# Moving the attention block's fold and raising its DVE steps in a fused attention and convolution kernel

## The chip, the cores and the metric

The kernel runs on one core of a Trainium2 chip. The metric is device microseconds of one execution of the whole program. Five engines work side by side, each on its own list of instructions in a fixed order: TensorE (PE, with the weight loads shown apart as PEld), VectorE (DVE), ScalarE (ACT), GpSimd (POOL) and SyncE (SP, which issues most of the DMAs). An instruction that waits for a semaphore holds up all that stands behind it in its engine's list.

## The reference

`x` is 8 images of 384 channels and 64 by 64 tokens, float32. Two layers follow each other, each with a residual:

```python
def _L0_conv_ref(x, Wq, bq, Wk, bk, Wv, bv, Wfc, bfc):
    q = apply_rope_2d(conv1x1(x, Wq, bq))
    k = apply_rope_2d(conv1x1(x, Wk, bk))
    v = conv1x1(x, Wv, bv)
    q = jax.nn.elu(to_heads(q) * scale) + 1.0          # 6 heads of 64
    k = jax.nn.elu(to_heads(k)) + 1.0
    kv = jnp.einsum('bhnd,bhne->bhde', k, to_heads(v))
    k_sum = k.sum(axis=2)
    normalizer = jnp.einsum('bhnd,bhd->bhn', q, k_sum)[..., None]
    out = jnp.einsum('bhnd,bhde->bhne', q, kv) / (normalizer + 1e-06)
    return conv1x1(out, Wfc, bfc)
...
x = x + _L0_conv_ref(_gn(x), ...)   # group norm, 32 groups, no affine part
x = x + _L1_conv_ref(_gn(x), ...)   # 1x1, filter on 8x8 FFT patches, depthwise 3x3, gelu gate, 1x1
```

## The kernel before

An image `b` is worked on in 8 bands `j` of 512 tokens; a band is a tile of 128 partitions by 3 channel tiles by 512. Two stages alternate. In the first, `queries(b, ...)`, the attention of image `b` is finished: for each band `q_project` makes the queries (matmuls `pq` L599, rotation on DVE L611, L626, L628, then elu as two activations on ACT L337, L338 and a DVE step L339), `q_normalise` multiplies them with the key sums (`pn` L637) and inverts (DVE L645, L646, and a split in two bfloat16 parts by ACT casts L650, L652 and DVE L651, L653), `q_spread` brings the inverse to all channels (`prb` L661) and multiplies it in (DVE L670, four steps for a band), and `project_out` multiplies with the folded matrix `mt` (`pf` L678) and adds to `x` (L682). In the second stage, the loop over bands of layer 1, the keys and values of image `b + 1` are projected and summed up in the accumulator `acc` (L470) in between the matmuls of layer 1, so that at its end `acc` holds the sum of key times value, and the sum of keys, of every head. The last band's depthwise taps of the image before (`late`, ACT L780, DVE L799, contraction L832, L843) run inside `queries`.

What is called the block here is `kv_finish_heads` (images 1 to 7): it reads `acc`, copies the key sums out (L567), has POOL spread them into `ks_bd` (`key_sums`, twelve copies L498), writes `kvt_bd` by six DVE steps (L572), two for each of three channel tiles, turns the three tiles on PE (`pt` L584), copies the result to `kvt` on ACT (L585) and, in `fold`, multiplies with `wfc` (`pm` L508); nine ACT copies (L515) then place it in `mt`. Image 0 has a function of its own, `kv_finish`, with other steps before the same `fold`; there four of the nine copies are on DVE (L513).

`kv_finish_heads` is a generator. `queries` steps it once after each third of band 1's query projection (the order of the three `pq` is 2, 0, 1), and then has

```python
        next(late, None)
        if b:
            run(finish)
        normalise(0)
        run(q_project(b, 2, wq, qbias, q))
```

so that `pn` of band 0 is recorded behind the fold. Later `normalise(j + 1)` stands between the projections of band `j + 2`. A third chain, `layer0_chain(b + 1, ...)`, is stepped once or twice for every band: it is the group norm of the next image, whose steps are small matmuls (`ps_m`, `ps_mc`, `ps_v`, `ps_r`, L273 and L281) and small DVE steps on 32 partitions (L301, L304, L307 to L310 make `rsg`, which `ps_r` reads). It runs for images 1 to 7, during the queries of images 0 to 6.

The order of the instructions on each engine is made when the program is built: a scheduler goes by the recorded order and by priorities, and inside `with tc.high_priority():` an instruction goes ahead of others that are ready. PSUM is one pool of eight banks, so a matmul group also waits for the last reader of the bank it gets.

Of the kernel before, what the change touches and what calls it, by code (L numbers as in the profile page):

```python
# [12 lines left out]
ALU = mybir.AluOpType  # L13

P = 128
C = 384
CT = 3
# [6 lines left out]
HD = 64  # L24
# [93 lines left out]
def conv_blocks_kernel(ctx: ExitStack, tc: tile.TileContext, a: dict, out: bass.AP, nb: int):  # L118
    nc = tc.nc
# [9 lines left out]
    def ps_tile(name):  # L129
        return psum.tile([P, 512], F32, tag="ps", name=name)  # L130

    def w_tile(shape, name):
        return work.tile(shape, F32, tag="w", name=name)
# [6 lines left out]
    def load_x(b, j):  # L140
        if b >= nb:
            return
        t = xp.tile([P, CT, BT], F32, tag="x", name=f"x_{b}_{j}")
        nc.sync.dma_start(t, x_in[b][:, :, j * BT : (j + 1) * BT])
        xt[b, j] = t
# [102 lines left out]
    halves = (slice(0, 64), slice(64, P))  # L248
# [3 lines left out]
    kvt_bd = const.tile([P, CT, P], F32, tag="kvt_bd", name="kvt_bd")  # L252
# [239 lines left out]
    def key_sums(kx, column):  # L492

        for c0, at, n in QRUNS:

            for s in range(0, n, 32):
                h, c, q = (c0 + s) // HD, c0 + s, at + s
                nc.gpsimd.tensor_copy(  # L498
                    ks_bd[q % P : q % P + 32, q // P, h : h + 2 * NH + 1 : NH],
                    kx[c % P : c % P + 32, c // P, column : column + 1].to_broadcast([32, 3]),  # L500
                )

    def fold(b, kvt, wfc, done):

        mt = small.tile([P, CT, C], F32, tag="mt", name=f"mt_{b}", bufs=1)
        for t in range(CT):
            pm = ps_tile(f"pm_{b}_{t}")
            nc.tensor.matmul(pm[:, :C], kvt[:, t, :], wfc[:, t, :], start=True, stop=True)  # L508
            for i, (c, at, n) in enumerate(QPIECES):
                if c // P == t:  # L510
                    dst, src = mt[at % P : at % P + n, at // P, :], pm[c % P : c % P + n, :C]
                    if i % 2 and not b:
                        nc.vector.tensor_copy(dst, src)  # L513
                    else:
                        nc.scalar.copy(dst, src)  # L515
        done.append(mt)
# [46 lines left out]
    def kv_finish_heads(b, acc, vb, wfc, done):  # L563

        kx = acc[:, : CT * (HD + 1)].rearrange("p (m d) -> p m d", m=CT)
        sums = small.tile([P, CT, 1], F32, tag="key_sums", name=f"key_sums_{b}")
        nc.vector.tensor_copy(sums, kx[:, :, HD:])  # L567
        key_sums(sums, 0)
        for m in range(CT):
            for h in range(2):  # L570
                head = 2 * m + h
                nc.vector.scalar_tensor_tensor(  # L572
                    kvt_bd[halves[h], m, halves[h]],
                    vb[halves[h], head * HD : (head + 1) * HD],
                    kx[halves[h], m, HD : HD + 1],
                    kx[halves[h], m, :HD],
                    ALU.mult,
                    ALU.add,
                )
        yield  # L580
        kvt = w_tile([P, CT, P], f"kvt_{b}")
        pt = ps_tile(f"pt_{b}")
        for m in range(CT):
            nc.tensor.transpose(pt[:, m * P : (m + 1) * P], kvt_bd[:, m, :], ident)  # L584
        nc.scalar.copy(kvt, pt[:, : CT * P].rearrange("p (m k) -> p m k", m=CT))  # L585
        yield
        yield
        fold(b, kvt, wfc, done)

# [42 lines left out]
    def q_normalise(b, j, q):  # L632

        pn = ps_tile(f"pn_{b}_{j}")
        for t in range(CT):
            for s in range(4):
                nc.tensor.matmul(  # L637
                    pn[32 * s : 32 * s + 32, :P],
                    ks_bd[:, t, :],
                    q[:, t, s * P : (s + 1) * P],  # L640
                    start=(t == 0),
                    stop=(t == CT - 1),
                )
        rn = small.tile([P, P], F32, tag="rn", name=f"rn_{b}_{j}")
        nc.vector.tensor_scalar_add(rn, pn[:, :P], 1e-6)  # L645
        nc.vector.reciprocal(rn, rn)  # L646

        part = small.tile([P, P], BF16, tag="part", name=f"part_{b}_{j}")
        parts = small.tile([P, P], BF16, tag="parts", name=f"parts_{b}_{j}")
        nc.scalar.copy(part, rn)  # L650
        nc.vector.scalar_tensor_tensor(rn, part, take_off[:, 0:1], rn, ALU.mult, ALU.add)  # L651
        nc.scalar.copy(part, rn)  # L652
        nc.vector.scalar_tensor_tensor(parts, part, take_off[:, 1:2], rn, ALU.mult, ALU.add)  # L653
        return parts

    def q_spread(b, j, q, rn):
        pr = [ps_tile(f"prb_{b}_{j}_{s}") for s in range(4)]
        for t in range(CT):
            for s in range(4):
                strip = slice(32 * s, 32 * s + 32)  # L660
                nc.tensor.matmul(  # L661
                    pr[s][:, t * P : (t + 1) * P],
                    expand[strip, t * P : (t + 1) * P],
                    rn[strip, :],
                    start=True,
                    stop=True,
                )
        for s in range(4):
            qq = q[:, :, s * P : (s + 1) * P]
            nc.vector.tensor_mul(qq, qq, pr[s][:, :C].rearrange("p (t n) -> p t n", t=CT))  # L670
# [196 lines left out]
    def layer0_chain(b, prepared):  # L867

        if b >= nb:
            return  # L870
        wk = load_weight(b, "wk", k_runs) if b else first_wk
        params = []
        if b == 0:
            sum_weight(wk, "wk")
        yield from norm_chain(b, 0, params)
        scale_weight(wk, params)
        yield
        prepared += params, wk, k_bias(b, params)
# [5 lines left out]
    def run(*chains):  # L884

        chains = list(chains)
        while chains:
            chains = [c for c in chains if next(c, chains) is not chains]
# [65 lines left out]
    def queries(b, keys, before_last, late):  # L954


        wq, qbias = keys.wq, keys.qbias
        q, done, normaliser = {}, [], {}

        def normalise(j):  # L960
            normaliser[j] = q_normalise(b, j, q[j])

        run(q_project(b, 0, wq, qbias, q))
        before_last()
        run(keys.accumulate(NBAND - 1))
        next(late, None)
        finish = keys.finish(done)
        for _ in zip(q_project(b, 1, wq, qbias, q), finish):
            pass
        prepared = []  # L970
        chain = layer0_chain(b + 1, prepared)

        next(late, None)
        if b:
            run(finish)
        normalise(0)
        run(q_project(b, 2, wq, qbias, q))
        run(finish)
        mt = done[0]
        q_spread(b, 0, q[0], normaliser.pop(0))  # L980
        project = q_project(b, 3, wq, qbias, q)
        next(project)
        normalise(1)
        run(project)
        run(project_out(b, 0, q.pop(0), mt))
        q_spread(b, 1, q[1], normaliser.pop(1))
        normalise(2)
        for j in range(2, NBAND):
            if j < NBAND - 2:
                project = q_project(b, j + 2, wq, qbias, q)  # L990
                for _ in range(2):
                    next(project)
                normalise(j + 1)
                run(project)
                next(chain, None)
            q_spread(b, j, q[j], normaliser.pop(j))
            output_ = project_out(b, j - 1, q.pop(j - 1), mt)
            if j == NBAND - 2:
                next(output_)
                normalise(j + 1)  # L1000
            run(output_)
            if j < NBAND - 2:
                next(chain, None)
            if j in (5, 7):
                load_x(b + 1, j // 6)
            next(late, None)
        run(chain)
        run(project_out(b, NBAND - 1, q.pop(NBAND - 1), mt))
        return prepared
# [24 lines left out]
    take_off = const.tile([P, 2], F32, tag="take_off", name="take_off")  # L1034
# [62 lines left out]
    before_last, late = nothing, iter(())  # L1097
    for b in range(nb):
        prepared = queries(b, keys, before_last, late)
        keys = Keys(b + 1, prepared)  # L1100
        params = []
# [16 lines left out]
        for j in range(NBAND):  # L1118
# [5 lines left out]
            h = normalised(b, j, params, (8, 8), "f") if j else ahead  # L1124
# [26 lines left out]
        def before_last(b=b):  # L1151
            contract(b, NBAND - 2)
# [6 lines left out]
    h = ahead  # L1159
    for j in range(NBAND):  # L1160
# [4 lines left out]
        if j < NBAND - 1:  # L1165
            h = normalised(b, j + 1, params, (8, 8), "f")
# [52 lines left out]
```

## Time and profile before

| | |
|---|---|
| time, median of 3 runs | 3357.73 us (3355.45 to 3360.14) |
| the profiled execution's own time | 3356.93 us |
| its span in the profile | 3354.8 us |
| mean granted clock of PE | 0.994 |
| busy: PE, DVE, ACT | 98%, 82%, 61% of the span |

A row of the timeline gives the start and the length of an instruction, or of a run of like ones, in us from the start of the span, then the engine, the line, what is written and read, the size and the count; brackets give the idle time ahead of it and what ended it. A float32 matmul leaves two records, so `x6` is one group of three. A row's length includes some 0.1 us that the next instruction already overlaps, so steps are better taken from start to start. The granted clock is the share of its full clock that PE was given.

### The profile page before, as it was taken

To read this page: it belongs to the slowest core of one execution; us is meant where nothing else is said; L and a number is where in the kernel's file an instruction comes from. 1 tells how busy PE (TensorE), PEld (TensorE's weight loads), DVE (VectorE), ACT (ScalarE), POOL (GpSimd) and SP (SyncE) were. 2 spreads that over 40 slices of the span, in tenths; PEclk is the share of its full clock that TensorE was granted. 3 is DMA by queue.
4 is the path that set the end of the run, shared out by engine and by line. 5 is a ranking of instruction groups with operands and counts; after the bars stand their busy time and mean duration, and the time that the engine had idled before them with its cause. 6 is when DMAs were issued, how large, how long until landed. Compare 5 with 4: busy or idle time off the path is not lost.

```text
span 3354.8 us, 53523 instructions
## 1 busy us (share of the span) xinstructions
PE 3293.9 (98%) x21370; PEld 1850.3 (55%) x21370; DVE 2752.8 (82%) x4524; ACT 2032.8 (61%) x4032; POOL 134.2 (4%) x261
## 2 busy tenths in 40 slices
PE   8999999999999999999999999999999999999987
PEld 5544566456654566545665456654566445664454
DVE  7577789967889688896888968898788977989698
ACT  4445666566665566655666656656576665556563
POOL 0000000000010000100001000000000000000000
PEclk9999999999999999999999999999999999999999
DMA  6323335342443423534335343443333431324113
GB/s 223 107 95 99 95 80 128 110 137 67 109 113 113 137 67 95 129 110 120 86 83 133 108 121 76 103 132 107 103 96 95 133 117 52 86 70 126 58 25 52
DMA packets 151502, 343.37 MB, mean 102 GB/s; under 512 B 27365, under 2 KB 38613, under 8 KB 143061
## 3 DMA queue, kind: packets, MB, share of 16 engines
q1 hardware_dynamic: 123844, 282.85, 25.1%
q0 software_dynamic: 27216, 56.89, 11.3%
q8 instruction: 168, 2.75, 0.3%
q14 instruction: 82, 0.66, 0.1%
q10 hardware_dynamic: 192, 0.21, 0.0%
HBM read 232.70 MB, written 99.88 MB: 99 GB/s over the span
## 4 chain that ended last, share of the span: by engine, by line
PE 78%; DVE 14%; ACT 5%; issue 2%; DMA 0%; SPq 0%; DVEq 0%; ACTq 0%
PE pk L438 14%; PE pi L696 14%; PE pf L678 13%; PE pv L454 13%; PE pq L599 7%; DVE dw L799 5%; PE pw L832 4%; PE pb L731 3%; PE pd L710 2%; PE pw L843 2%; PE acc L470 2%; PE acc L483 2%; DVE qc L611 1%; ACT qs L620 1%; DVE qs L611 1%
## 5 line engine op out<-in xcount | busy, mean ns | idle before, releaser
L799 DVE SCALAR_TENSOR_TENSOR dw<-ring,w_dw,dw 128x512 f32<-128x512 f32 x1401 | 977.9, 747 | 244.5 <-ACT ring L747 205.4
L438 PE MATMUL pk<-wk,x 128*128 128x384 f32 x1536 | 544.1, 495 | 0.0
L599 PE MATMUL pq<-x,wq 128*128 128x512 f32 x1152 | 524.7, 603 | 2.6 <-ACT mt L515 2.6
L696 PE MATMUL pi<-w_in,hf 128*128 128x384 f32 x1536 | 514.8, 492 | 1.3 <-ACT hf L332 1.3
L678 PE MATMUL pf<-qc,mt 128*128 128x512 f32 x1152 | 510.7, 597 | 0.0
L454 PE MATMUL pv<-wv,x 128*128 128x384 f32 x1344 | 470.0, 488 | 0.0
L696 PEld LDWEIGHTS pi<-w_in,hf 128*128 128x128 f32 x1536 | 288.6, 191 | 196.1 <-issue 4.1
L438 PEld LDWEIGHTS pk<-wk,x 128*128 128x128 f32 x1536 | 283.1, 190 | 204.8 <-issue 31.6
L461 ACT COPY v<-pv 128x384 f32<-128x384 f32 x224 | 108.7, 485 | 424.5 <-PE pv L454 423.3
L678 PEld LDWEIGHTS pf<-qc,mt 128*128 128x128 f32 x1152 | 214.3, 190 | 255.5 <-issue 243.4
L454 PEld LDWEIGHTS pv<-wv,x 128*128 128x128 f32 x1344 | 253.6, 190 | 181.4 <-issue 8.4
L599 PEld LDWEIGHTS pq<-x,wq 128*128 128x128 f32 x1152 | 210.9, 191 | 247.1 <-issue 227.0
L682 DVE SCALAR_TENSOR_TENSOR x<-pf,bfc,x 128x512 f32<-128x512 f32 x192 | 139.0, 745 | 92.3 <-PE pf L678 92.1
L337 ACT ACTIVATE qs<-qc 128x512 f32<-128x512 f32 (+1 forms) x128 | 107.0, 836 | 171.3 <-DVE qc L628 171.3
L179 ACT ACTIVATE differences<-x,shift 128x512 f32<-128x512 f32 x168 | 120.2, 716 | 120.6 <-DVE x L682 120.6
L832 PE MATMUL pw<-gated,w_out 128*128 128x256 f32 x768 | 179.4, 383 | 0.0
L441 DVE TENSOR_TENSOR kc<-pk,kbias 128x384 f32<-128x384 f32 x256 | 140.8, 550 | 39.3 <-PE pk L438 39.2
L703 ACT COPY ht<-pi 128x384 f32<-128x384 f32 x256 | 115.1, 482 | 91.6 <-PE pi L696 88.2
L832 PEld LDWEIGHTS pw<-gated,w_out 128*128 128x128 f32 x768 | 146.7, 192 | 37.1 <-issue 6.5
L337 ACT ACTIVATE ks<-kc 128x1536 f32<-128x1536 f32 x64 | 95.0, 1485 | 98.5 <-DVE kc L445 97.7
L862 POOL DMA_DIRECT2D out_dram<-y x63 | 80.7, 1280 | 1811.2 <-ACT y L857 1004.7
L332 ACT ACTIVATE hf<-x,nb,rs 128x512 f32<-128x512 f32 x192 | 146.4, 808 | 2.4 <-DVE nb L315 2.3
(178 smaller groups left out, 4407.2 us busy)
## 6 DMA issues: line engine op xcount, KB each, us to landing
tq<-in_tq SPq DMA_DIRECT2D x64, 1024.0 KB, 4.8
x<-in_x SPq DMA_DIRECT2D x64, 768.0 KB, 6.0
tk<-in_tk SPq DMA_DIRECT2D x64, 768.0 KB, 4.4
out_dram<-x SPq DMA_DIRECT2D x63, 768.0 KB, 3.3
out_dram<-y POOLq DMA_DIRECT2D x63, 768.0 KB, 7.8
xs<-in_x SPq DMA_DIRECT2D x56, 768.0 KB, 5.8
dw<-tap POOLq DMA_DIRECT2D x14, 512.0 KB, 7.4
wk<-in_wk SPq DMA_DIRECT2D x8, 576.0 KB, 3.9
```

Of the source, the lines that this page charges most:

```text
L179: nc.scalar.activation(out[:, m, :], x_[:, m, :], AF.Identity, bias=shift[:, m : m + 1], accum_out=of_m[0])
L332: nc.scalar.activation(dst, src, AF.Identity, bias=nb_[:, t : t + 1], scale=rs[:, t : t + 1])
L337: nc.scalar.activation(e, x_, AF.Relu, scale=-1.0)
L438: nc.tensor.matmul(pk[:, :C], tokens(t), wks[:, t, :], start=(t == 0), stop=(t == CT - 1))
L441: nc.vector.tensor_add(kc[:, i, :], pk[:, :C], bias)
L454: nc.tensor.matmul(pv[:, :C], xt[b, j][:, t, i * P : (i + 1) * P], wvs[:, t, :], start=(t == 0), stop=(t == CT - 1),)
L599: nc.tensor.matmul(p_, wqs[:, t, m * P : (m + 1) * P], xt[b, j][:, t, :], start=(t == 0), stop=(t == CT - 1),)
L678: nc.tensor.matmul(p_, mt[:, t, m * P : (m + 1) * P], q[:, t, :], start=(t == 0), stop=(t == CT - 1))
L682: nc.vector.scalar_tensor_tensor(xm, p_, bfc[:, m : m + 1], xm, ALU.add, ALU.add)
L696: nc.tensor.matmul(p_[:, :C], h[:, t, i * P : (i + 1) * P], w_in[:, t, :], start=(t == 0), stop=(t == CT - 1),)
L799: nc.vector.scalar_tensor_tensor(acc[:, m], src, wd, acc[:, m], ALU.mult, ALU.add)
L832: nc.tensor.matmul(p_[h][:, m - m0, :], w_out[:, 0, m * P : (m + 1) * P], gated[:, h * HT : (h + 1) * HT], start=(m == m0), stop=False,)
```

## The change

Three things are changed. In `kv_finish_heads` the six steps L572 are recorded ahead of the POOL copies and get the highest priority, and one `yield` moves from behind the transpositions to ahead of them, so that `pt` is recorded after all three `pq` of band 1. In `q_normalise` the two DVE steps of the inverse, and the casts and steps of its split, get the highest priority, for every band of every image. In `queries`, `normalise(0)` is recorded ahead of `run(finish)`, and so ahead of the fold.

```diff
         sums = small.tile([P, CT, 1], F32, tag="key_sums", name=f"key_sums_{b}")
         nc.vector.tensor_copy(sums, kx[:, :, HD:])
+        with tc.high_priority():
+            for m in range(CT):
+                for h in range(2):
+                    head = 2 * m + h
+                    nc.vector.scalar_tensor_tensor(
+                        kvt_bd[halves[h], m, halves[h]],
...
+                    )
         key_sums(sums, 0)
-        for m in range(CT):
-            for h in range(2):
...
+        yield
         yield
         kvt = w_tile([P, CT, P], f"kvt_{b}")
         pt = ps_tile(f"pt_{b}")
         for m in range(CT):
             nc.tensor.transpose(pt[:, m * P : (m + 1) * P], kvt_bd[:, m, :], ident)
         nc.scalar.copy(kvt, pt[:, : CT * P].rearrange("p (m k) -> p m k", m=CT))
-        yield
         yield
         fold(b, kvt, wfc, done)
...
         rn = small.tile([P, P], F32, tag="rn", name=f"rn_{b}_{j}")
-        nc.vector.tensor_scalar_add(rn, pn[:, :P], 1e-6)
-        nc.vector.reciprocal(rn, rn)
-
+        with tc.high_priority():
+            nc.vector.tensor_scalar_add(rn, pn[:, :P], 1e-6)
+            nc.vector.reciprocal(rn, rn)
         part = small.tile([P, P], BF16, tag="part", name=f"part_{b}_{j}")
         parts = small.tile([P, P], BF16, tag="parts", name=f"parts_{b}_{j}")
-        nc.scalar.copy(part, rn)
-        nc.vector.scalar_tensor_tensor(rn, part, take_off[:, 0:1], rn, ALU.mult, ALU.add)
-        nc.scalar.copy(part, rn)
-        nc.vector.scalar_tensor_tensor(parts, part, take_off[:, 1:2], rn, ALU.mult, ALU.add)
+        with tc.high_priority():
+            nc.scalar.copy(part, rn)
+            nc.vector.scalar_tensor_tensor(rn, part, take_off[:, 0:1], rn, ALU.mult, ALU.add)
+            nc.scalar.copy(part, rn)
+            nc.vector.scalar_tensor_tensor(parts, part, take_off[:, 1:2], rn, ALU.mult, ALU.add)
         return parts
...
         next(late, None)
+        normalise(0)
         if b:
             run(finish)
-        normalise(0)
         run(q_project(b, 2, wq, qbias, q))
```

## The prediction

> **What bounds the kernel now.** I read the page first: PE is busy all the time, so only time in which PE waits can be won, and whatever makes PE wait is paid in full.
>
> ```profile
> PE 3293.9 (98%) x21370; PEld 1850.3 (55%) x21370; DVE 2752.8 (82%) x4524; ACT 2032.8 (61%) x4032; POOL 134.2 (4%) x261
> ```
>
> Then PE's list of waits (total us, times, longest). The change aims at the first and third of these rows, 14.3 us together; the second belongs to the group norm chain, and it will matter.
>
> ```profile
> PE pt L584 <- DVE kvt_bd L572: 9.7, 13, 1.3
> PE ps_r L281 <- DVE rsg L310: 5.2, 9, 2.4
> PE prb L661 <- DVE parts L653: 4.6, 7, 0.7
> PE pq L599 <- ACT mt L515: 2.6, 1, 2.6
> ```
>
> Third, PE's timeline where image 1's block lies. Images 2 to 6 repeat it to 0.1 us every 408.3 us.
>
> ```profile
> 582.49 5.42 PE L599 MATMUL pq<-x,wq 128*128 128x512 f32 x12
> 587.74 0.27 PE L584 MATMUL pt<-groups,kvt_bd 128*128 128x128 f32 x1
> 589.28 0.33 PE L584 MATMUL pt<-groups,kvt_bd 128*128 128x128 f32 x1 [1.27 <-DVE kvt_bd L572]
> 589.91 0.33 PE L584 MATMUL pt<-groups,kvt_bd 128*128 128x128 f32 x1 [0.29 <-DVE kvt_bd L572]
> 590.07 2.74 PE L599 MATMUL pq<-x,wq 128*128 128x512 f32 x6
> 592.65 2.10 PE L508 MATMUL pm<-wfc,kvt 128*128 128x384 f32 x6
> 594.68 0.86 PE L637 MATMUL pn<-qc,ks_bd 128*32 128x128 f32 x24
> 595.47 7.99 PE L599 MATMUL pq<-x,wq 128*128 128x512 f32 x18
> ...
> 612.67 2.74 PE L678 MATMUL pf<-qc,mt 128*128 128x512 f32 x6
> ```
>
> Last, the DVE and PE timelines where the group norm chain of the next image ends, and the granted clock in two windows after image 0's wait of 2.58 us. The columns of a window are busy time by engine, then PE's clock (0.88, 0.81).
>
> ```profile
> 664.23 0.29 DVE L645 TENSOR_SCALAR rn<-pn 128x128 f32<-128x128 f32 x1 [1.32 <-PE pn L637]
> ...
> 666.77 0.14 DVE L310 TENSOR_TENSOR rsg<-rsg,y 32x1 f32<-32x1 f32 x1
> 666.83 0.33 DVE L651 SCALAR_TENSOR_TENSOR rn<-part,take_off,rn 128x128 f32<-128x128 bf16 x1
> 667.10 0.73 DVE L611 SCALAR_TENSOR_TENSOR qs<-pq,qbias,tq 128x512 f32<-128x512 f32 x1
> 667.76 0.33 DVE L653 SCALAR_TENSOR_TENSOR parts<-part,take_off,rn 128x128 bf16<-128x128 bf16 x1
> 668.02 0.67 DVE L626 TENSOR_TENSOR qs<-qs,sq 128x512 f32<-128x512 f32 x1
> ```
> ```profile
> 666.96 0.60 PE L281 MATMUL ps_r<-rsg,of_group 32*128 32x1 f32 x4
> ```
> ```profile
> 200.00:203.00 3.00, 0.42 (x12) 0.19 (x2) 2.91 (x6) 2.90 (x5) 0.00 (x0) 0.88 0.40 164
> 203.00:210.00 7.00, 7.00 (x14) 3.06 (x15) 6.46 (x14) 1.54 (x4) 0.00 (x0) 0.81 0.00 0
> ```
>
> **The order that the change makes.** I compared the orders of the two built programs, engine by engine. No matmul is added or removed. In images 1 to 7 PE's order pq, pq, pt, pq, pm, pn becomes pq, pq, pq, pt, pn, pm. DVE does all six L572 ahead of L339 (128x1024). ACT casts `part` in between the copies of `mt`, and does band 1's elu behind all nine copies. On SP one load changes places with a neighbour in each image; POOL's order stays.
>
> **Part 1, the wait at pt: gain.** PE ends the second pq at 587.65 (twelve records of 0.43). The third pq then runs at once (2.58), then pt (0.57 with its gaps: pt starts at 590.32 and ends for the next at 590.80). L572 is done by 586.78 + 6 x 0.30 = 588.6, so nothing is waited for. pn takes 0.79 to 591.59; its inputs, L339 (588.6 + 1.23) and POOL's twelve copies (586.93 + 3.56 = 590.49), are there. The copy of kvt on ACT (0.48 from 590.97) is hidden by pn. pm takes 2.03, so band 2's pq starts at 593.65 instead of 595.47: -1.82 for each of images 1 to 6. In image 7 pt starts at 3037.69 and the pq after it at 3038.70, a wait shorter by 1.3, so -0.5 there. The first prb waited some 0.26 for parts: gone as well.
>
> **Part 2, what is late next: band 0's pf.** It needs all four L670 of band 0. ACT works without a gap from the end of pt, by its rows from start to start: kvt 0.50, two L620 1.41, four mt copies 1.94, tap 0.66, part 0.32, tap 0.66, mt 0.49, part 0.32, four mt 1.94, L620 0.71, L337 0.66, L620 0.70, L338 0.54, L337 1.08, L338 1.06. That is 12.99: band 1's elu input is ready at 590.97 + 12.99 = 603.96, against 600.59 before. DVE waits too: L645 now stands behind one L611 and waits for pn (from 590.4 to 591.7), with the rest of band 1's rotation queued behind it, on which ACT's elu waits; and the two part steps wait for the casts. So L339 of band 1 ends at 605.23. PE would be at band 1's pn at 606.62 - 2.08 = 604.54 and waits 0.75. DVE goes on: L339 1.14, two L611 1.32, two L628 1.74, L645 0.20, L670 0.47, L646 0.86, L670 0.47, L339 0.60, to 610.80; the next L339 needs ACT's last L338 of band 2, at 610.85 (L628's end 608.28, then 0.97, 0.54, 1.06); then L339 1.14, L651 0.26, L670 0.50, L653 0.26, L670 0.55 end at 613.59. PE is ready for pf at 605.29 + 0.79 + 5.26 = 611.34 and waits 2.26. pf starts at 613.6 instead of 612.67: what pt gave is gone, and 0.93 more. Bounds: if ACT and DVE were quick enough, 0; if each cast costs one further step of 0.66 to 0.75, 3.7 in all. I keep 2.26, which is made of rows.
>
> **Part 3, the later steps.** Parts of band 2 are ready at some 626.9 (L646 now runs from 623.7), and prb wants them at 631: its wait of 0.65 goes, in images 1 to 7. The load of band 3's `tq` waits for the last L611 of band 1, now near 598.2; it is needed at 613.5, and the issue table has 4.8 us to landing. The tap on POOL is 3 us later, and its readers come after 640.
>
> **Part 4, ps_r: loss.** In images 1 to 6 L645 of band 5 now stands ahead of L304, and L651, one L611, L653 and L626 ahead of L309 and L310. L645 still waits for pn at 664.23. So rsg comes later by L304 0.06, L651 0.27, L611 0.66, L653 0.26, L626 0.60: 1.85. PE stands at ps_r, with prb and pf behind it, where it waited 0.1 to 0.2 already: +1.85 in each of six images. In image 0 the order differs by one step, and PE's next pq (2.58) covers that.
>
> The Trainium skill ("VectorE: DVE Perf Modes", The DRAIN you can't avoid) has every DVE step followed by a flush of about its length less 266 ns. The rows differ: L611 is 0.74 long and the next starts 0.66 later. By the page part 4 would be some 3 us an image; the rows decide.
>
> **Part 5, image 0.** By the same walk L645 of band 1 frees a bank at 201.8, where PE waited for a copy of mt until 202.81, and pf starts near 207.8 instead of 209.49: -1.7, which includes the slow clock after the old wait (twelve pq took 6.84 instead of 5.42).
>
> **The sum.** Images 1 to 6: -1.82 - 0.26 + 0.75 + 2.26 - 0.65 + 1.85 = +2.13 each, 12.8. Image 7, without part 4: -0.5 - 0.26 + 0.75 + 2.26 - 0.65 = +1.6. Image 0: -1.7. Together +12.7.
>
> **The clock.** The two windows say that a wait of 2.58 us cost 1.42 more. In layer 1 of the last image PE waits of 2.14, 2.28, 2.57 and 3.52 us are followed by such stretches, one of 1.99 is not, nor are the 1.27 and 0.29 at pt. My thirteen new waits are 2.0 (ps_r) and 2.26 (pf), at the edge. Bounds 0 and 13 x 1.42 = 18.5; I take none at ps_r, nearest to 1.99, and three of seven at pf, nearest to 2.14 and 2.28 but between large matmuls: +4.3.
>
> The skill ("TensorE: Matmul & The Clock Gate", Why this matters for your kernels) sets the limit at idle gaps of about 3 us, which leaves this term at 0. The row after 2.58 us speaks against it.
>
> So 12.7 + 4.3 = 17.0 on the profiled execution's 3356.93 is 3373.9; the median before lies 0.8 higher, and the forecast is 3374.7. A difference within 0.2% (6.7 us) is about what a measurement of this kernel can't tell from no change.
>
> **The rivals.**
> - *No wait at pf* (the faster one). If the last L670 ends before 611.3, ACT's chain being shorter by 2.3, images 1 to 6 have -1.82 - 0.26 - 0.65 + 1.85 = -0.88, image 7 -1.4, image 0 -1.7: -8.4, 3349. For it: ACT is busy only 61% of the span. Against: every item of its chain is a row, and it has no gap. 0.07.
> - *No loss at ps_r*: 12.7 - 11.1 = +1.6, 3359. It needs rsg's steps to run ahead, against the built order. 0.07.
> - *Neither*: -8.4 - 11.1 = -19.5, 3338. The change would do just what its words say. 0.04.
> - *Most new waits slow the clock*: ten or more of thirteen, +14 to +18 instead of +4.3: 3385 to 3389. 0.08.
> - *The forecast*, both waits and none to nine slow stretches: 3370 to 3383, and from 3366 where the wait at pf is 0.6 shorter in each of seven images: 0.74.
>
> The range 3359 to 3384 takes in the forecast and the second rival. Faster by over 0.2% is the first and third rivals, 0.11; within 0.2% is the second and the forecast's low edge, 0.10; slower 0.79.
>
> **What would show it.** In the changed profile: no wait of PE at pt; waits near 0.7 at band 1's pn and 2.3 at band 0's pf on L670 (seven times); none at prb; waits near 2.0 at ps_r, six times; in image 0 the wait for mt shorter. If pf shows no wait, part 2 is wrong; if ps_r keeps 0.2, part 4 is; if all stand and the time is under 3366 or over 3384, the clock is.

## The result, and the profile after

The changed kernel takes 3382.7 us (median of 6 runs, 3377.9 to 3384.3), the kernel before 3357.97 beside it: a ratio of 1.0071, 95% interval 1.0058 to 1.0084. It is slower by 0.7%. The profiled execution took 3382.57 us (before: 3356.93), its span is 3380.8 us, the mean granted clock 0.990 (before: 0.994).

The page's first part shows the same instructions on every engine, and 11 us more of busy time on PE, with no matmul added: some matmuls took longer.

```profile
PE 3305.1 (98%) x21370; PEld 1853.4 (55%) x21370; DVE 2755.2 (81%) x4524; ACT 2030.9 (60%) x4032; POOL 134.7 (4%) x261
```

PE's list of waits (total, times, longest) has lost pt and prb, which the change aimed at, and has gained pf and pn; ps_r's total has tripled. These three rows hold 34.7 us; the rows pt, ps_r and prb of before held 19.5.

```profile
PE ps_r L281 <- DVE rsg L310: 15.3, 13, 1.9
PE pf L680 <- DVE qc L672: 14.8, 7, 2.1
...
PE pn L638 <- DVE qc L339: 4.6, 7, 0.7
```

PE's timeline at image 1's block. (Lines from L584 on stand one or two lower in the changed file: L680 is pf, L672 the spread's multiplication, L663 prb, L638 pn, L600 pq, L586 pt.) The block itself now runs through without a wait, as it was meant to. The waits come later, at band 1's pn and band 0's pf.

```profile
579.74 7.99 PE L600 MATMUL pq<-x,wq 128*128 128x512 f32 x18
587.57 0.49 PE L586 MATMUL pt<-groups,kvt_bd 128*128 128x128 f32 x3
587.99 0.86 PE L638 MATMUL pn<-qc,ks_bd 128*32 128x128 f32 x24
588.78 2.20 PE L508 MATMUL pm<-wfc,kvt 128*128 128x384 f32 x6
...
602.42 0.86 PE L638 MATMUL pn<-qc,ks_bd 128*32 128x128 f32 x24 [0.66 <-DVE qc L339]
603.21 5.42 PE L600 MATMUL pq<-x,wq 128*128 128x512 f32 x12
610.74 7.96 PE L680 MATMUL pf<-qc,mt 128*128 128x512 f32 x18 [2.11 <-DVE qc L672]
```

The same pf, 18 records of the same shape after the same wait, one image later, and the pf behind image 1's wait at ps_r: 9.66 and 9.69 us instead of 7.96. These are the longer matmuls.

```profile
1022.78 9.66 PE L680 MATMUL pf<-qc,mt 128*128 128x512 f32 x18 [2.11 <-DVE qc L672]
```
```profile
666.22 0.60 PE L281 MATMUL ps_r<-rsg,of_group 32*128 32x1 f32 x4 [1.86 <-DVE rsg L310]
...
667.16 9.69 PE L680 MATMUL pf<-qc,mt 128*128 128x512 f32 x18
```

Windows of the changed kernel around the two waits at pf, laid on the 3.41 us grid on which the granted clock changes (last section). A row has the stretch, its length, then the busy time of PE, PEld, DVE, ACT and POOL, PE's clock, and the DMA share. In image 2 the whole wait (1020.67 to 1022.78) lies in one stretch of 3.41 us, in which PE is busy for 1.30, and the next stretch is granted half the clock. In image 1 the same wait lies across an edge, PE is busy for 1.68 in the first part, and the clock stays at 1.00.

```profile
606.95:610.36 3.41, 1.68 (x4) 0.38 (x2) 3.35 (x7) 1.42 (x3) 0.00 (x0) 1.00 0.20 82
610.36:613.78 3.42, 3.04 (x7) 1.44 (x8) 3.42 (x7) 0.00 (x0) 0.00 (x0) 1.00 0.02 5
1019.96:1023.37 3.41, 1.30 (x4) 0.38 (x3) 3.41 (x7) 0.45 (x2) 0.00 (x0) 1.00 0.00 0
1023.37:1026.79 3.42, 3.42 (x6) 1.34 (x5) 3.42 (x6) 0.00 (x0) 0.00 (x0) 0.50 0.02 5
```

Eight such half-clock stretches (slow stretches below) lie in the queries of images 1 to 7: five after the six waits at ps_r, three after the seven at pf. The kernel before has none there, and one in image 0, which in this execution of the changed kernel is gone.

**Where the 24.5 us up to the last image's layer 1 come from** (its wait at ps_r ends at 3173.27 before and 3197.73 after). Image 1's band 1 starts 2.75 earlier (start-up and image 0; most of it is luck, see part 5 below). The one image without a slow stretch takes 410.3 us from ps_r to ps_r (1491.99 to 1902.32) against 408.3: +2.0 in each of images 1 to 6, 12.0. Eight slow stretches at 9.66 - 7.96 = 1.70: 13.6. That leaves 1.6 for image 7. The last layer 1 adds some 1.5; it has one slow stretch more than before.

### The profile page after: what moved, and what is told of

Same layout as the page of the kernel before. It is cut to its first block, busy times and chain, and to the rows that moved or that the text cites. A ratio compares the mean times of both kernels' runs of the same rounds, so it can differ in the third digit from the quotient of the medians.

```text
span 3380.8 us, 53510 instructions
## 1 busy us (share of the span) xinstructions
PE 3305.1 (98%) x21370; PEld 1853.4 (55%) x21370; DVE 2755.2 (81%) x4524; ACT 2030.9 (60%) x4032; POOL 134.7 (4%) x261
## 3 DMA queue, kind: packets, MB, share of 16 engines
q8 instruction: 168, 2.75, 0.3%
## 4 chain that ended last, share of the span: by engine, by line
PE 89%; DVE 6%; ACT 4%; DMA 0%; issue 0%; SPq 0%; DVEq 0%; ACTq 0%
PE pf L680 15%; PE pk L438 14%; PE pi L698 14%; PE pv L454 13%; PE pq L600 11%; PE pw L834 5%; PE pb L733 3%; PE pw L845 3%; PE acc L470 3%; PE pd L712 2%; PE acc L483 2%; DVE dw L801 2%; PE pn L638 1%; ACT mt L515 1%; ACT qs L338 1%; ACT qs L621 1%
## 5 line engine op out<-in xcount | busy, mean ns | idle before, releaser
L680 PE MATMUL pf<-qc,mt 128*128 128x512 f32 x1152 | 524.8, 611 | 14.8 <-DVE qc L672 14.8
L600 PE MATMUL pq<-x,wq 128*128 128x512 f32 x1152 | 521.4, 601 | 2.0 <-DVE rn L647 2.0
L680 PEld LDWEIGHTS pf<-qc,mt 128*128 128x128 f32 x1152 | 218.3, 194 | 281.5 <-issue 265.1
L600 PEld LDWEIGHTS pq<-x,wq 128*128 128x128 f32 x1152 | 211.0, 190 | 249.5 <-issue 229.5
```

The costliest lines, as they stand in the source:

```text
L600: nc.tensor.matmul(p_, wqs[:, t, m * P : (m + 1) * P], xt[b, j][:, t, :], start=(t == 0), stop=(t == CT - 1),)
L680: nc.tensor.matmul(p_, mt[:, t, m * P : (m + 1) * P], q[:, t, :], start=(t == 0), stop=(t == CT - 1))
```

## The experiments

The theory (A) was that of the prediction: the loss is made of waits, at ps_r by the priority of band 5's inverse, at pn and pf by that of the first bands, and of the clock that these waits slow. The rivals were that moving pt and the fold is itself the loss (B), and that the slow stretches have another cause (C).

**The moves without the priority of the inverse.**

```diff
-        with tc.high_priority():      # both places in q_normalise
+        with nullcontext():
```

> The changed kernel with the highest priority taken out of the inverse and its split (q_normalise) alone; the block's steps stay first, pt stays behind the third pq and pn ahead of the fold. Theory A (the loss is the priority of the inverse: it delays rsg ahead of ps_r and puts casts and DVE steps ahead of band 1's elu, and both waits slow PE's clock): no wait at pt; ps_r back at 0.1 to 0.2; the wait at pf falls from 2.11 to 0.3 to 1.0, since in the built order the two casts stand behind band 1's elu; band 2's prb waits its old 0.65 again; no slow stretches in the queries of images 1 to 7. Per image -1.82 at pt, +0.7 at pf: -1.1, so 3345 to 3351 beside 3358 for the kernel before. Rival B (the moves are the loss: with pt behind the third pq, ACT's nine copies of mt push band 1's elu back and pf waits whoever does the casts): the wait at pf stays at 1.8 or more in seven images, 3358 to 3366.

Measured: 3351.8 us, ratio to the kernel before 0.9980 (0.9972 to 0.9989). pf does not wait at all, ps_r does not wait in the queries either, and no slow stretch is left in images 1 to 7. So B falls: without the priority the new order is faster than the kernel before, and it is the priority that turns this into a loss. The time lies just above A's 3345 to 3351. What I did not expect is a wait of 1.40 at band 0's prb, since the casts of its split now stand on ACT behind band 1's elu:

```profile
601.18 0.34 PE L663 MATMUL prb<-parts,expand 32*128 32x128 bf16 x12 [1.40 <-DVE parts L655]
...
610.27 6.17 PE L680 MATMUL pf<-qc,mt 128*128 128x512 f32 x14
```

**The priority alone,** on the kernel before (the diff's part in `q_normalise` and nothing else).

> The kernel before with only the highest priority in q_normalise added; block, pt, pn and fold stay where they were. Theory A: pt keeps its waits (9.7 in all), ps_r waits 1.8 to 2.0 in six images (+1.75 each, 10.5), about half to five sixths of these are followed by a slow stretch (3 to 5 of 1.7, 5 to 8.5), prb loses its seven waits of 0.65 (-4.6), image 0 gains 1 to 2; the wait at pf stays under 0.7. Sum +9 to +14: 3367 to 3372. Rival B: the priority costs little, under 3 us; 3355 to 3361, and ps_r stays near 0.2.

Measured: 3368.4 us, ratio 1.0030 (1.0018 to 1.0041). The total came out as A had it, by other terms: ps_r waits 1.14, not 1.8 to 2.0, and pf waits 1.02, where I had under 0.7. One slow stretch lies in images 1 to 7, not three to five. The loss is shown; its size at each place depends on the rest of the order: the priority costs 10.3 on the order before and 30.9 on the moved one (3382.7 against 3351.8).

**Band 5 without the priority.**

```diff
-        with tc.high_priority():
+        with tc.high_priority() if j != 5 else nullcontext():
```

> The changed kernel, but the inverse of band 5 alone without the priority. On DVE rsg's steps then stand as in the kernel before; ACT and PE keep the changed order. Theory A: ps_r waits 0.1 to 0.2, pf 2.1 and pn 0.66 as in the changed kernel (seven times), three slow stretches or so (after pf alone). Against the changed kernel -6 x 1.7 = -10.2 of waiting and -5 x 1.7 = -8.5 of clock: 3382.7 - 18.7 = 3364, range 3361 to 3367. Rival C (the slow stretches do not come from the waits at ps_r, but move elsewhere or stay): -10 alone, 3372 to 3374.

Measured: 3366.5 us, ratio 1.0024 (1.0014 to 1.0033). The waits at pf (2.11) and pn (0.67) are untouched, those at ps_r are gone from the queries. It is 16.2 us under the changed kernel. The waits give 6 x 1.83 = 11.0 (PE goes from the last pq to ps_r in 2.87, not 4.70, from start to start); the profile has five slow stretches up to the last image, against eight, for 5.1. Rival C (the waits alone) falls. Four of the five stand behind waits at pf, one in image 0.

**PE kept busy in the waits,** so that only the clock can differ.

```diff
+    def filler(p_, wanted): [nc.tensor.matmul(p_[:, :C], w_in[:, 0, :P], w_in[:, 1, :], start=True, stop=True) for _ in range(2 * wanted)]
...
+            filler(p_, 0 < b < nb - 1 and (j, m) == (6, 1))   # ahead of this pq
...
+            filler(p_, b > 0 and (j, m) == (0, 0))            # ahead of this pf
```

> The changed kernel with 26 matmuls of no use added (two of 128x384 each, some 0.7 apiece, into a bank that the next group overwrites): ahead of band 6's last pq in images 1 to 6, so that PE comes to ps_r 1.4 later, and ahead of band 0's first pf in images 1 to 7. All else keeps its order on every engine. They lie in time in which PE waited, so the ends of the waits stay where they were; only PE's idle time shrinks, from 1.86 to 0.4 and from 2.11 to 0.7. Theory A with the clock (a stretch of idle PE time is what slows its clock): none of the eight slow stretches is left in the queries of images 1 to 7, and the time falls by 8 x 1.7 = 13.6 to 3369 (3366 to 3372), though the kernel does more work. Rival C (the clock is slowed by something else): eight or so stay, 3381 to 3385.

Measured: 3370.6 us, ratio 1.0036 (1.0024 to 1.0048), whose interval lies wholly under the changed kernel's. It does 26 matmuls more and is 12.1 us faster. All eight slow stretches are gone (image 0 has one in this execution, which the changed kernel's profile lacks, so that eight at 1.70 less that one leave some 12), and image 2's pf, at the place where it took 9.66, takes 7.99:

```profile
1022.13 1.45 PE L590 MATMUL pf<-w_in 128*128 128x384 f32 x4
1024.31 7.99 PE L680 MATMUL pf<-qc,mt 128*128 128x512 f32 x18 [0.73 <-DVE qc L672]
```

So PE's idle time slows its clock, and this was about half of the 24.7 us.

**Which bands.** Three kernels keep the moves and differ in the bands `j` whose inverse is raised: `j > 1 and j != 5`, then with band 0 too (`j not in (1, 5)`), or with band 1 too (`j not in (0, 5)`).

> The changed kernel, with the priority of the inverse and its split left only to bands 2, 3, 4, 6 and 7 (none for bands 0, 1 and 5). It tells which bands' priority cost the time. Theory A (band 5 costs at ps_r, bands 0 and 1 cost at pn and pf, the others gain): waits as in the run with the moves alone, 1.40 at band 0's prb, none at pf and pn, 0.2 at ps_r, but band 2's prb no longer waits its 0.41: 3351.8 - 7 x 0.41 = 3349 (3346 to 3352). Rival D (the priority costs in the other bands too, since it pushes other DVE steps back): 3353 or more.

> The kernel with the priority in bands 2, 3, 4, 6 and 7, and band 0 raised as well. Theory A: band 0's steps alone put its two casts in between the copies of mt, and pn of band 1 waits its 0.66 again, seven times; band 0's prb loses its 1.40; on DVE the four L672 then follow band 2's rotation directly, without steps of band 1 between them: 602.4 + 4.96 = 607.3, while PE comes to pf at 608.5: no wait at pf. -0.74 in each of seven images, and image 0 better by 1 to 2: 3350.5 - 6.5 = 3344 (3341 to 3348). Rival H (band 0's casts are enough for the wait at pf): pf waits 1.5 or more, 3352 to 3364.

> The same, but band 1 raised instead of band 0. Theory A: band 1's four DVE steps and the larger L339 stand between band 0's L672, whose last ends at 606.7 + 5.2 = 611.9 where PE comes to pf at 610.3: a wait of 1.6 at pf, too short to slow the clock, and prb keeps its 1.40: 3350.5 + 7 x 1.6 = 3362 (3358 to 3366). Rival H: pf waits under 0.5, 3349 to 3354.

Measured: 3350.5 (ratio 0.9977, 0.9968 to 0.9986), 3344.7 (0.9961, 0.9949 to 0.9974) and 3359.5 (1.0006, 0.9997 to 1.0015). Raising the late bands takes band 2's prb wait away. Raising band 0 takes its prb's 1.40 and gives 0.67 at pn, with no wait at pf. Raising band 1 gives the wait at pf that was worked out, 1.61, and no slow stretch after it. Rival H falls both times: the wait at pf in the changed kernel needs band 1's DVE steps in between band 0's L672, and band 0's priority on top only makes it longer (2.11 with both). Image 0, which A had better by 1 to 2 when band 0 is raised, is not: its pq waits 3.19, with bands 0 and 1 both left alone 2.57.

```profile
608.09 0.86 PE L638 MATMUL pn<-qc,ks_bd 128*32 128x128 f32 x24 [0.67 <-DVE qc L339]
608.88 5.42 PE L600 MATMUL pq<-x,wq 128*128 128x512 f32 x12
614.14 7.89 PE L680 MATMUL pf<-qc,mt 128*128 128x512 f32 x18
```
```profile
613.24 4.96 PE L680 MATMUL pf<-qc,mt 128*128 128x512 f32 x11 [1.61 <-DVE qc L672]
```

**The block's steps alone,** on the kernel before: the six L572 first and raised, and nothing else.

> The kernel before with one part of the change alone: the six steps L572 ahead of the POOL copies and with the highest priority; pt, pn and fold stay where they were. PE comes to pt at 587.7 in the first image with a block; the six steps end near 588.6. Theory A: the wait at pt shrinks from 1.56 to 0.5 to 1.0 an image, -0.5 to -1.0 in each of seven, and nothing else moves: 3351 to 3355. Rival E (only the move of pt takes the wait away, the priority is nothing): 3357 to 3359. Rival F (L339 of band 0, pushed back by four steps, hurts): above 3359.

Measured: 3349.0 us, ratio 0.9975 (0.9964 to 0.9985). pt waits a single 0.29 in place of 1.57, better than A had it. The part of the change that is worth most is its smallest one, and it needs no move. Moving pt and the fold on top of it brought no gain: the run with the moves alone has these six steps too and takes 3351.8, with 1.81 us of bracketed waits in an image's queries (1.40 and 0.41) against 0.94 here (0.29 and 0.65).

```profile
586.59 0.63 PE L585 MATMUL pt<-groups,kvt_bd 128*128 128x128 f32 x2
587.52 0.33 PE L585 MATMUL pt<-groups,kvt_bd 128*128 128x128 f32 x1 [0.29 <-DVE kvt_bd L572]
```

**A later prb, and two combinations.** The first takes the moves without the priority and lets band 0's prb come after the first third of band 3's projection; the second adds the priority for band 2, and in image 0 for all bands but 5; the third has the same priorities with the block's steps alone, pt, fold and prb unmoved.

```diff
-        q_spread(b, 0, q[0], normaliser.pop(0))
         project = q_project(b, 3, wq, qbias, q)
         next(project)
+        q_spread(b, 0, q[0], normaliser.pop(0))
```
```diff
+        with tc.high_priority() if j == 2 or not b and j != 5 else nullcontext():
```

> The moves alone (no priority in q_normalise), and band 0's prb recorded one third of a projection (three matmuls, 2.6 us) later. On PE nothing else changes, DVE and ACT keep their order. In the run with the moves alone prb waited 1.40 for parts and the last L672 ended 1.1 before pf. Theory A: the wait of 1.40 goes, pf then waits 0.3 to 0.5 on L672: -0.9 to -1.1 in each of seven images, 3351.8 - 7 = 3345 (3343 to 3347). Rival G (the wait only moves, since L672 is bound by prb): pf waits 1.4, 3350 to 3353.

> The kernel with the later prb, and the priority of the inverse for band 2 alone in images 1 to 7 and for all bands but 5 in image 0. Theory A: band 2's prb loses its 0.41 (seven images, -2.9), image 0's wait at pq falls from 2.58 to 1.99 (-0.6 to -2, with the clock): 3345 - 4 = 3341 (3338 to 3344), about 0.5% under the kernel before and 1.2% under the changed one. Rival D (priority costs elsewhere): 3345 or more.

> The kernel before, with the six steps L572 first and raised (pt, pn, fold and prb stay where they were), and the priority of the inverse for band 2 in images 1 to 7 and for all bands but 5 in image 0. Theory A: 3349 as with the block's steps alone, less band 2's 0.65 in seven images (-4.6) and 1 to 2 in image 0: 3343 (3340 to 3346), as fast as the best so far, with neither pt nor the fold moved. Rival I (band 2's raised steps delay something in this order): 3347 or more.

Measured: 3350.9 (0.9979, 0.9970 to 0.9988), 3342.4 (0.9955, 0.9942 to 0.9967) and 3344.3 (0.9957, 0.9945 to 0.9970). In the first, A was right about pf (0.46) and wrong about the sum: band 2's prb, which had waited 0.41, now waits 1.06, so that of 1.40 only 0.3 is won. With band 2 raised that wait is gone, and the second kernel is the fastest: 0.45% under the kernel before, with 0.47 at pf as the only bracketed wait in the queries of image 1. The third can't be told from it, nor can the late bands and 0 (3344.7).

```profile
594.27 10.46 PE L600 MATMUL pq<-x,wq 128*128 128x512 f32 x24
...
611.68 7.99 PE L680 MATMUL pf<-qc,mt 128*128 128x512 f32 x18 [0.47 <-DVE qc L672]
```

PE's waits in the queries of one of images 1 to 6, in us, as PE's timeline brackets them, beside the medians (a dash: none bracketed):

| kernel | us | pt | prb 0 | pn 1 | pf 0 | prb 2 | ps_r |
|---|---|---|---|---|---|---|---|
| before | 3358.0 | 1.57 | - | - | - | 0.65 | - |
| changed | 3382.7 | - | - | 0.66 | 2.11 | - | 1.86 |
| moves alone | 3351.8 | - | 1.40 | - | - | 0.41 | - |
| priority alone | 3368.4 | 1.57 | - | - | 1.02 | - | 1.14 |
| changed, not band 5 | 3366.5 | - | - | 0.67 | 2.11 | - | - |
| late bands | 3350.5 | - | 1.39 | - | - | - | - |
| late bands and 0 | 3344.7 | - | - | 0.67 | - | - | - |
| late bands and 1 | 3359.5 | - | 1.39 | - | 1.61 | - | - |
| block's steps alone | 3349.0 | 0.29 | - | - | - | 0.65 | - |
| later prb | 3350.9 | - | - | - | 0.46 | 1.06 | - |
| combined | 3342.4 | - | - | - | 0.47 | - | - |
| block's steps, band 2 | 3344.3 | 0.29 | - | - | - | - | - |
| changed, with fillers | 3370.6 | - | - | 0.67 | 0.73 | - | 0.57 |

## Why the prediction was right, and which term was too small

The forecast was 3374.7 and the time is 3382.7. Sign and mechanism were right, and every new wait stands where the walk had put it.

- Part 1: no wait at pt, and the first prb follows 7.82 after its pq (8.10 before, from start to start).
- Part 2: pn waits 0.66 (0.75 was worked out) and pf 2.11 (2.26). ACT's chain from the end of pt to band 1's last elu step is 12.95 long (588.07 to 601.02; 12.99).
- Part 3: band 2's prb does not wait.
- Part 4: PE comes to ps_r 1.83 later (from the start of the last pq 4.70, not 2.87; 1.85 was worked out). That PE had waited 0.1 to 0.2 there already was misread: the 0.19 in the list is layer 1's own ps_r. On DVE, L655 and L627 stand ahead of L309 and L310 as the built order had it. The flush that the Trainium skill ("VectorE: DVE Perf Modes", The DRAIN you can't avoid) describes would have made some 3 us of this, an estimate; the section itself says that a next step that is not held starts earlier, which the prediction left out. The measured 1.83 sides with the rows.

```profile
665.10 0.33 DVE L655 SCALAR_TENSOR_TENSOR parts<-part,take_off,rn 128x128 bf16<-128x128 bf16 x1
665.36 0.13 DVE L309 TENSOR_SCALAR y<-y 32x1 f32<-32x1 f32 x1
665.43 0.67 DVE L627 TENSOR_TENSOR qs<-qs,sq 128x512 f32<-128x512 f32 x1
666.02 0.14 DVE L310 TENSOR_TENSOR rsg<-rsg,y 32x1 f32<-32x1 f32 x1
```

- Part 5: pf of image 0 started at 206.67 instead of 207.8, a gain of 2.8, not 1.7; most of it is luck. Some 0.9 was there long before these queries (the first L483 starts at 55.38, before at 56.25): the half clock at the start of the span lasted 6.83 us, before 10.24. Some 1.3 more is the slow stretch that this execution lacks. What the change itself gives is a wait of 1.98 in place of 2.58. In three other runs (priority alone, not band 5, fillers) the same wait of 1.99 is followed by a slow stretch, and from its first pn to its first pf image 0 takes 23.50; it is 23.82 in the kernel before and 21.87 in the changed one.
- The sum without the clock: +2.0 an image measured, +2.13 worked out.
- **The step that failed is the clock.** "I take none at ps_r" and three at pf made +4.3. It is 8 x 1.70 = 13.6, three at pf as forecast and five at ps_r. Three things were off. I priced a stretch at 1.42, from a row in which the stretch had begun before the wait ended (the granted clock fell at 202.31, the wait ended at 202.81); filled with matmuls it costs half of its 3.41. I took the wait at ps_r for 2.0 us of idle time, nearest to the 1.99 that was not followed; but PE goes from the end of pq to the first pf at 667.16 with ps_r's one-column matmuls and a short prb only: 1.86 + 0.94 = 2.8. And I went by the length of the wait, where its place decides: waits of the same 2.11 were followed by a slow stretch three times and not four times. The 1.99 that I went by lies across an edge of the grid, with 1.1 in the larger part.

The rival of ten or more slow stretches out of thirteen was nearer to the truth than the three of my sum; eight was still in the forecast's own bounds, at their upper end.

## What to carry to other kernels

The highest priority for a chain that is late in one place is paid wherever the same code runs: look in the built order for what each raised step overtakes, above all a short chain such as rsg on which PE waits, and raise only where the wait is (here band 2). Before reordering, try the smallest part alone: putting six DVE steps first gave a quarter of a per cent by itself, and all that came on top of it in the change lost 1%. Where PE is the bound, price a new wait of about 2 us by its length and by the half-clock stretch that may follow, some 1.7 us more.

## What the runs showed of the hardware

In every profile here the edges at which the granted clock changes lie whole multiples of 3.4133 us apart (668.39 to 1023.37 is 354.98, or 104 of them; 1023.37 to 1081.40 is 17), and the phase differs from one execution to the next. Laid over PE's waits, this grid sorts the waits at pf without exception (a cell is one piece of 3.41 us of it): in the changed kernel and the one without band 5, the seven that had 2.10 to 2.11 in one cell were followed by a cell at half clock, the seven with 1.26 to 1.99 were not, nor were those with 1.61 in the kernel that raises band 1. With the 2.8 us of little work taken as idle, ps_r fits too: five cells with 2.19 to 2.80 were followed by a slow one, that with 1.93 was not; with the priority alone, that with 2.08 was, and the five with 1.14 to 1.74 were not. Two places do not fit. At image 0's wait at pq 1.99 in one cell was enough in four runs, which at pf it was not. And in the last image's layer 1, where many matmuls are small (64 by 64), idle time alone does not sort: in the kernel that raises band 1, a cell with PE busy for 1.44 (3215.57 to 3218.98) was not followed by a slow one, and a cell with 2.01 (3277.01 to 3280.42) was. So something near 2.0 of 3.41 us decides in the queries, and what decides in that layer 1 stays open. That idle time in a wait is the cause is shown by the kernel with fillers; the exact limit, and how much a small matmul counts, is only read from these rows.

The Trainium skill ("TensorE: Matmul & The Clock Gate", Part 1: The HAM clock gate) describes a free-running activity window of 3413 ns, which agrees with the grid measured here. I had not weighed it in the prediction. The same page (Why this matters for your kernels) warns of idle gaps over about 3 us; here waits of 1.86 and 2.11 were enough, where that limit would have left the 13.6 us out.
